# A normalized convolution over 8 images: x laid out by row and column parity, four full products per 2x2 pixel block

## The chip, the cores and the metric

The kernel runs on one core of a Trainium2 chip. The metric is the time of one execution on the device in microseconds (us), the median of several runs. Of the core's engines, TensorE (PE in the profile) multiplies matrices into PSUM and loads its weights by records of their own (PEld); VectorE (DVE) and ScalarE (ACT) work on elements; GpSimd (POOL) prepares constants; SyncE (SP) issues transfers. Sixteen DMA engines move the data.

## The reference

`x` is 8 images of 32 channels of 128 x 128 f32. `_gn` normalizes over 16 groups of two channels each; `_L0_conv_ref` convolves by transforms; the result is added to `x`:

```
def _gn(v, G=16, eps=1e-5):
    g = v.reshape(B_, G, C_ // G, H_, W_)
    m = jnp.mean(g, axis=(2, 3, 4), keepdims=True)
    s = jnp.var(g, axis=(2, 3, 4), keepdims=True)
    return ((g - m) / jnp.sqrt(s + eps)).reshape(v.shape)
def _L0_conv_ref(x, weight, bias, stride, padding):
    ...  # transforms of 256 x 256, norm='ortho'
    sh = (fft_H - out_h) // 2
    sw = (fft_W - out_w) // 2
    out = sp[:, :, sh:sh + out_h, sw:sw + out_w]
    return out + bias[None, :, None, None]
x = x + _L0_conv_ref(_gn(x), L0_conv_weight, L0_conv_bias, 1, 1)
```

The three 'ortho' transforms leave a factor of 1/256, and the crop starts at (64, 64). So with g the normalized x, `out[h, w] = x[h, w] + bias + 1/256 * sum weight[c, a, b] * g[c, 64+h-a, 64+w-b]` over channels and the 3 x 3 taps, where g is zero outside of the image. The sum reads rows and columns 62 to 127 of g and is empty for h > 65 or w > 65: only a 66 x 66 corner of each output gets a convolution, the rest is x + bias.

## The kernel before

Four images (4 x 32 channels) lie on the 128 partitions at a time, so there are two passes (`grp`, L119). All of x fits on the chip: its ten loads, five chunks of rows (CHUNKS, L54) for each pass, are issued first on the SP queue (L72). The weights come in four copies on ScalarE's queue (L80) and are put by GpSimd into block-diagonal matrices `w_bd` of 128 x 128, one for each of the nine taps (L86); three quarters of each matrix are zeros.

Each pass takes statistics of 512 elements at a time with `bn_stats` (L113, 32 instructions), joins them with `bn_aggr` (L132), and goes back and forth between engines: mean of the two channels of a group by a product with `pair` (L137), copied out and subtracted (L139, L141), variance (L143), again a product (L147), square root on ScalarE (L150), reciprocal (L152). VectorE then writes the normalized part g (L158). ScalarE adds the bias where the convolution gives nothing (L171, L175), and those rows are stored (L179).

The convolution goes block by block, each of six output rows x 66 columns = 396 elements in a PSUM bank: nine products accumulate (L192), then VectorE adds bias and x (L200). Eleven blocks make a pass. In the first pass the statistics of the second are spread behind the blocks' additions (L205). A chunk's rows are stored when its last block has been added (L206). A scheduler of the language may move instructions of an engine past each other; the lists further down show the order that results.

Of the kernel before, what the change touches and what calls it, by code (L numbers as in the profile page):

```python
# [12 lines left out]
The 1/256 is part of the normalization's factor, where it is exact.  # L13
"""
# [14 lines left out]
STATS = 512  # most elements that one bn_stats takes  # L29
BLOCK = 6  # output rows of one accumulation group in PSUM  # L30
# [3 lines left out]
def conv_preact_kernel(  # L34
# [9 lines left out]
    B, C, H, W = x.shape  # L44
    K = 3
    IMGS = P // C
    NGRP = B // IMGS
    LO = (FFT - H) // 2 - (K - 1)  # first row and column of g that the sum reads
    N = H - LO  # rows and columns that the sum reads
    NC = H + K - 1 - (FFT - H) // 2  # output rows and columns where it isn't empty  # L50
    NP = N + K - 1  # with the zeros behind the image
    # rows of the image in one load and store: a multiple of 4 (bn_stats), and chunks that
    # hold output rows of the convolution start at a multiple of BLOCK
    CHUNKS = ((0, 24), (24, 24), (48, 20), (68, 32), (100, 28))  # L54
    NSTAT = H * W // STATS
    RSTAT = STATS // W

    cpool = ctx.enter_context(tc.tile_pool(name="const", bufs=1))
    xpool = ctx.enter_context(tc.tile_pool(name="x", bufs=2))
    gpool = ctx.enter_context(tc.tile_pool(name="g", bufs=2))  # L60
# [4 lines left out]
    # all of x fits on the chip: its loads are issued at once  # L65
    xts = []
    for grp in range(NGRP):
        src = x[grp * IMGS : (grp + 1) * IMGS].rearrange("b c h w -> (b c) h w")
        tiles = []
        for i, (r0, rows) in enumerate(CHUNKS):  # L70
            xt = xpool.tile([P, rows, W], F32, tag=f"x{i}", name=f"x{grp}_{i}")
            nc.sync.dma_start(xt, src[:, r0 : r0 + rows, :])  # L72
            tiles.append(xt)
        xts.append(tiles)

    # weights and bias, once for each image on the partitions
    w_sb = cpool.tile([P, K * K, C], F32, name="w_sb")
    bias_sb = cpool.tile([P, 1], F32, name="bias_sb")
    for b in range(IMGS):
        nc.scalar.dma_start(w_sb[b * C : (b + 1) * C], weight)  # L80
        nc.scalar.dma_start(bias_sb[b * C : (b + 1) * C], bias)
    w_bd = cpool.tile([P, K * K, P], F32, name="w_bd")
    nc.gpsimd.memset(w_bd, 0.0)  # L83
    for b in range(IMGS):
        part = slice(b * C, (b + 1) * C)
        nc.gpsimd.tensor_copy(w_bd[part, :, part], w_sb[part])  # L86
# [3 lines left out]
    nc.gpsimd.memset(pair, 0.5)  # L90
# [8 lines left out]
    pair2 = pair.rearrange("p a b -> p (a b)")  # L99
    eps = cpool.tile([P, 1], F32, name="eps")  # L100
    nc.gpsimd.memset(eps, EPS * FFT * FFT)

    all_stats = [
        spool.tile([P, NSTAT, 6], F32, tag="stats", name=f"stats{grp}") for grp in range(NGRP)
    ]
    todo = [
        [(i, r0 // RSTAT, r) for i, (r0, rows) in enumerate(CHUNKS) for r in range(0, rows, RSTAT)]
        for _ in range(NGRP)
    ]

    def take_stats(grp, count):
        for i, s0, r in todo[grp][:count]:
            nc.vector.bn_stats(  # L113
                all_stats[grp][:, s0 + r // RSTAT, :],
                xts[grp][i][:, r : r + RSTAT, :].rearrange("p h w -> p (h w)"),
            )
        del todo[grp][:count]

    for grp in range(NGRP):  # L119
        tiles = xts[grp]  # L120
        dst = out[grp * IMGS : (grp + 1) * IMGS].rearrange("b c h w -> (b c) h w")

        # zeros behind the image
        g = gpool.tile([P, NP, NP], F32, tag="g", name=f"g{grp}")
        nc.gpsimd.memset(g[:, N:NP, :], 0.0)
        nc.gpsimd.memset(g[:, 0:N, N:NP], 0.0)

        # mean and variance of each channel
        take_stats(grp, NSTAT)
        stats = all_stats[grp]  # L130
        mv = spool.tile([P, 2], F32, tag="mv", name=f"mv{grp}")
        nc.vector.bn_aggr(mv, stats.rearrange("p n s -> p (n s)"))  # L132
# [3 lines left out]
        ps_m = ps_stat.tile([P, 1], F32, tag="ps_m", name=f"ps_m{grp}")  # L136
        nc.tensor.matmul(ps_m, pair2, mv[:, 0:1], start=True, stop=True)  # L137
        mean = spool.tile([P, 1], F32, tag="mean", name=f"mean{grp}")
        nc.vector.tensor_copy(mean, ps_m)  # L139
        diff = spool.tile([P, 1], F32, tag="diff", name=f"diff{grp}")  # L140
        nc.vector.tensor_sub(diff, mv[:, 0:1], mean)  # L141
        var = spool.tile([P, 1], F32, tag="var", name=f"var{grp}")
        nc.vector.scalar_tensor_tensor(  # L143
            var, in0=diff, scalar=diff, in1=mv[:, 1:2], op0=ALU.mult, op1=ALU.add
        )
        ps_v = ps_stat.tile([P, 1], F32, tag="ps_v", name=f"ps_v{grp}")
        nc.tensor.matmul(ps_v, pair2, var, start=True, stop=True)  # L147
        # 1 / (256 * sqrt(var + eps))
        std = spool.tile([P, 1], F32, tag="std", name=f"std{grp}")
        nc.scalar.activation(std, ps_v, AF.Sqrt, bias=eps, scale=float(FFT * FFT))  # L150
        rstd = spool.tile([P, 1], F32, tag="rstd", name=f"rstd{grp}")
        nc.vector.reciprocal(rstd, std)  # L152

        # the part of x that the convolution reads, normalized
        for xt, (r0, rows) in zip(tiles, CHUNKS):
            lo = max(r0, LO)
            if lo < r0 + rows:
                nc.vector.tensor_scalar(  # L158
                    g[:, lo - LO : r0 + rows - LO, 0:N],
                    xt[:, lo - r0 : rows, LO:W],  # L160
                    mean,
                    rstd,
                    ALU.subtract,
                    ALU.mult,
                )

        # x + bias where the convolution gives nothing
        for xt, (r0, rows) in reversed(list(zip(tiles, CHUNKS))):
            nrc = min(max(NC - r0, 0), rows)
            if nrc:  # L170
                nc.scalar.activation(  # L171
                    xt[:, 0:nrc, NC:W], xt[:, 0:nrc, NC:W], AF.Identity, bias=bias_sb
                )
            if nrc < rows:
                nc.scalar.activation(  # L175
                    xt[:, nrc:rows, :], xt[:, nrc:rows, :], AF.Identity, bias=bias_sb
                )
            if not nrc:
                nc.sync.dma_start(dst[:, r0 : r0 + rows, :], xt)  # L179

        # x + (convolution + bias)
        for xt, (r0, rows) in zip(tiles, CHUNKS):
            nrc = min(max(NC - r0, 0), rows)
            if not nrc:
                continue
            for r in range(0, nrc, BLOCK):
                ps = ps_conv.tile([P, BLOCK, NC], F32, tag="ps", name=f"ps{grp}_{r0 + r}")
                for a in range(K):
                    for b in range(K):
                        top = r0 + r + K - 1 - a  # L190
                        left = K - 1 - b
                        nc.tensor.matmul(  # L192
                            ps,
                            w_bd[:, a * K + b, :],
                            g[:, top : top + BLOCK, left : left + NC],
                            start=(a == 0 and b == 0),
                            stop=(a == K - 1 and b == K - 1),
                        )
                part = xt[:, r : r + BLOCK, 0:NC]
# [34 lines left out]
```

## Time and profile before

| | us |
|---|---|
| median of 3 runs | 187.21 (186.94 to 187.78) |
| span of the profiled execution | 185.6 |
| TensorE busy | 137.0 |
| VectorE busy | 61.1 |
| ScalarE busy | 25.8 |

The span runs from the first to the last instruction of the profiled execution; the runs' times lie a little above it. Busy times of different engines overlap, so what decides is the chain of work that ended last, and the waits along it. In lists of grouped instructions a row gives line, engine, operation, output and inputs, and shapes, then the busy time in all, the mean time of one in ns, and the idle time of the engine before them with what ended it. In a table of stretches each engine has its busy time and, in brackets, its instructions; then follow the granted TensorE clock (1.00 is full), the share of the DMA engines' time and GB/s.

### The profile page before, as it was taken

To read this page: it belongs to the slowest core of one execution; us is meant where nothing else is said; L and a number is where in the kernel's file an instruction comes from. 1 tells how busy PE (TensorE), PEld (TensorE's weight loads), DVE (VectorE), ACT (ScalarE), POOL (GpSimd) and SP (SyncE) were. 2 spreads that over 40 slices of the span, in tenths; PEclk is the share of its full clock that TensorE was granted. 3 is DMA by queue.
4 is the path that set the end of the run, shared out by engine and by line. 5 is a ranking of instruction groups with operands and counts; after the bars stand their busy time and mean duration, and the time that the engine had idled before them with its cause. 6 is when DMAs were issued, how large, how long until landed. Compare 5 with 4: busy or idle time off the path is not lost.

```text
span 185.6 us, 1044 instructions
## 1 busy us (share of the span) xinstructions
PE 137.0 (74%) x404; PEld 78.0 (42%) x404; DVE 61.1 (33%) x102; ACT 25.8 (14%) x16; POOL 5.2 (3%) x17
## 2 busy tenths in 40 slices
PE   0000000249999999999999929999999999999960
PEld 0000000225555555555555515555555555555530
DVE  0258799599779611101110062101110011101110
ACT  0050200379700000000000029500000000000000
POOL 4230000000000000000000000000000000000000
PEclk9999999999999999999999996999999999999997
DMA  5689999997792052000440051990007000080006
GB/s 177 231 351 446 422 425 426 432 432 308 328 407 113 4 230 109 0 0 0 170 170 0 0 212 74 396 452 0 0 42 297 0 0 4 0 339 0 0 15 267
DMA packets 3268, 33.76 MB, mean 182 GB/s; under 512 B 576, under 2 KB 704, under 8 KB 704
## 3 DMA queue, kind: packets, MB, share of 16 engines
q1 hardware_dynamic: 2880, 33.56, 43.4%
q10 hardware_dynamic: 384, 0.15, 0.4%
q8 instruction: 3, 0.05, 0.1%
q14 instruction: 1, 0.01, 0.0%
HBM read 16.93 MB, written 16.78 MB: 182 GB/s over the span
## 4 chain that ended last, share of the span: by engine, by line
PE 74%; DMA 11%; DVE 9%; issue 1%; SPq 0%; ACT 0%; ACTq 0%
PE ps L192 73%; DMA x<-x_dram 11%; DVE stats L113 6%; DVE g L158 2%; DVE x L200 1%; DVE mv L132 1%; PE ps_v L147 1%; SPq L72 0%; PE ps_m L137 0%; ACT std L150 0%; DVE var L143 0%; DVE rstd L152 0%; DVE mean L139 0%; DVE diff L141 0%; ACT L150 0%
## 5 line engine op out<-in xcount | busy, mean ns | idle before, releaser
L192 PE MATMUL ps<-g,w_bd 128*128 128x396 f32 x396 | 135.4, 504 | 6.7 <-DVE g L158 6.7
L192 PEld LDWEIGHTS ps<-g,w_bd 128*128 128x128 f32 x396 | 76.3, 193 | 64.7 <-issue 9.9
L200 DVE SCALAR_TENSOR_TENSOR x<-ps,bias_sb,x 128x396 f32<-128x396 f32 x22 | 13.9, 630 | 103.2 <-PE ps L192 103.2
L113 DVE BATCH_NORM_STATS2 stats<-x 128x6 f32<-128x512 f32 x64 | 39.0, 679 | 12.3 <-DMA x<-x_dram 12.3
L137 PE MATMUL ps_m<-mv,pair 128*128 128x1 f32 x4 | 0.8, 278 | 32.8 <-DVE mv L132 32.8
L137 PEld LDWEIGHTS ps_m<-mv,pair 128*128 128x128 f32 x4 | 0.9, 250 | 33.1 <-issue 32.8
L175 ACT ACTIVATE x<-x,bias_sb 128x256 f32<-128x256 f32 (+2 forms) x6 | 14.5, 2483 | 0.0
L171 ACT ACTIVATE x<-x,bias_sb 128x1488 f32<-128x1488 f32 (+1 forms) x6 | 8.5, 1429 | 8.3 <-DVE stats L113 6.4
L150 ACT ACTIVATE std<-ps_v,eps 128x1 f32<-128x1 f32 x2 | 0.5, 261 | 59.6 <-PE ps_v L147 59.6
L158 DVE TENSOR_SCALAR g<-x,mean,rstd 128x396 f32<-128x396 f32 (+2 forms) x6 | 5.8, 1032 | 0.0
L150 ACT ACT_TABLE_LOAD x1 | 1.3, 1283 | 15.8 <-PE ps_v L147 15.8
L147 PE MATMUL ps_v<-var,pair 128*128 128x1 f32 x4 | 0.9, 304 | 2.8 <-DVE var L143 2.8
L171 ACT ACT_TABLE_LOAD x1 | 1.3, 1283 | 9.1 <-DMA bias_sb<-bias_dram 9.1
L132 DVE BATCH_NORM_AGGREGATE mv<-stats 128x2 f32<-128x192 f32 x2 | 2.0, 1022 | 0.1
L147 PEld LDWEIGHTS ps_v<-var,pair 128*128 128x128 f32 x4 | 0.8, 249 | 3.0 <-DVE var L143 1.7
L86 POOL COPY w_bd<-w_sb 32x288 f32<-32x288 f32 x4 | 1.7, 421 | 5.1 <-DMA w_sb<-weight_dram 5.0
L152 DVE RECIPROCAL rstd<-std 128x1 f32<-128x1 f32 x2 | 0.3, 164 | 2.5 <-ACT std L150 2.5
L83 POOL MEMSET w_bd<- 128x1152 f32 x1 | 1.1, 1058 | 0.3 <-POOLq L224 0.3
L95 POOL TENSOR_SCALAR_AFFINE_SELECT pair<-pair 128x128 f32<-128x128 f32 x1 | 0.7, 706 | 0.1
L91 POOL TENSOR_SCALAR_AFFINE_SELECT pair<-pair 128x128 f32<-128x128 f32 x1 | 0.7, 706 | 0.0
L139 DVE COPY mean<-ps_m 128x1 f32<-128x1 f32 x2 | 0.3, 153 | 0.7 <-PE ps_m L137 0.7
L143 DVE SCALAR_TENSOR_TENSOR var<-diff,mv 128x1 f32<-128x1 f32 x2 | 0.4, 212 | 0.0
(9 smaller groups left out, 1.9 us busy)
## 6 DMA issues: line engine op xcount, KB each, us to landing
x<-x_dram SPq DMA_DIRECT2D x4, 1536.0 KB, 13.9
out_dram<-x SPq DMA_DIRECT2D x4, 1536.0 KB, 5.1
x<-x_dram SPq DMA_DIRECT2D x2, 2048.0 KB, 22.3
out_dram<-x SPq DMA_DIRECT2D x2, 2048.0 KB, 8.2
x<-x_dram SPq DMA_DIRECT2D x2, 1792.0 KB, 24.9
out_dram<-x SPq DMA_DIRECT2D x2, 1792.0 KB, 6.6
x<-x_dram SPq DMA_DIRECT2D x2, 1280.0 KB, 17.9
out_dram<-x SPq DMA_DIRECT2D x2, 1280.0 KB, 4.4
```

Of the source, the lines that this page charges most:

```text
L83: nc.gpsimd.memset(w_bd, 0.0)
L86: nc.gpsimd.tensor_copy(w_bd[part, :, part], w_sb[part])
L113: nc.vector.bn_stats(all_stats[grp][:, s0 + r // RSTAT, :], xts[grp][i][:, r : r + RSTAT, :].rearrange("p h w -> p (h w)"),)
L132: nc.vector.bn_aggr(mv, stats.rearrange("p n s -> p (n s)"))
L137: nc.tensor.matmul(ps_m, pair2, mv[:, 0:1], start=True, stop=True)
L147: nc.tensor.matmul(ps_v, pair2, var, start=True, stop=True)
L150: nc.scalar.activation(std, ps_v, AF.Sqrt, bias=eps, scale=float(FFT * FFT))
L158: nc.vector.tensor_scalar(g[:, lo - LO : r0 + rows - LO, 0:N], xt[:, lo - r0 : rows, LO:W], mean, rstd, ALU.subtract, ALU.mult,)
L171: nc.scalar.activation(xt[:, 0:nrc, NC:W], xt[:, 0:nrc, NC:W], AF.Identity, bias=bias_sb)
L175: nc.scalar.activation(xt[:, nrc:rows, :], xt[:, nrc:rows, :], AF.Identity, bias=bias_sb)
L192: nc.tensor.matmul(ps, w_bd[:, a * K + b, :], g[:, top : top + BLOCK, left : left + NC], start=(a == 0 and b == 0), stop=(a == K - 1 and b ...
L200: nc.vector.scalar_tensor_tensor(part, in0=ps, scalar=bias_sb, in1=part, op0=ALU.add, op1=ALU.add)
```

## The change

The host now splits x by the parity of row and column: an image becomes 128 partitions (2 row parities x 2 column parities x 32 channels) of 64 x 64 elements. A partition pitch is 16 KiB in place of 64 KiB. One image fills the partitions, and there are eight images instead of two groups of four. In this layout an output pixel block of 2 x 2 needs input blocks at two row offsets and two column offsets, so the nine taps become four products with 128 x 128 matrices, which the host builds (`blocks`) and which hold the nine taps at several places; the output corner is 33 x 33 blocks, in three chunks of 11 x 33 = 363 elements. The first image is loaded in four transfers, the others in two; each is stored in two, and the host puts the output back in order.

The mean over a group is now over eight partitions (two channels x four parities) by a product with `avg`, which VectorE builds from `pair`. ScalarE loads its root table at the start (`warm`) and does the normalizing, as scale times x plus bias, for which VectorE also computes minus mean times reciprocal. ScalarE goes on to add the bias below (1,984 elements) and right (33 x 31). `tc.manual_schedule()` keeps the order as it is written. The core of the new code:

```diff
+    for img in range(B):
+        parts = 4 if img == 0 else 2
+        for k in range(parts):
+            rows = slice(k * H // parts, (k + 1) * H // parts)
+            nc.sync.dma_start(xts[img][:, rows, :], x[img, :, rows, :])
+        if img == 0:
+            nc.sync.dma_start(w_sb, weight)
+            nc.scalar.dma_start(bias_sb, bias)
...
+    warm = cpool.tile([P, 1], F32, name="warm")
+    nc.scalar.activation(warm, eps, AF.Sqrt)
...
+    def group_mean(img):
+        ps_ms[img] = ps_stat.tile([P, 1], F32, tag="ps_m", name=f"ps_m{img}")
+        nc.tensor.matmul(ps_ms[img], avg, mvs[img][:, 0:1], start=True, stop=True)
...
+    def normalize(img):
+        xt, g = xts[img], gs[img % 2]
+
+        std = spool.tile([P, 1], F32, tag="std", name=f"std{img}")
+        nc.scalar.activation(std, ps_vs[img], AF.Sqrt, bias=eps, scale=float(FFT * FFT))
+        rstd = spool.tile([P, 2], F32, tag="rstd", name=f"rstd{img}")
+        nc.vector.reciprocal(rstd[:, 0:1], std)
+        nc.vector.scalar_tensor_tensor(
+            rstd[:, 1:2], in0=means[img][:, 0:1], scalar=-1.0, in1=rstd[:, 0:1],
+            op0=ALU.mult, op1=ALU.mult,
+        )
+        nc.scalar.activation(
+            g[:, 0:N, 0:N], xt[:, LO:H, LO:W], AF.Identity,
+            bias=rstd[:, 1:2], scale=rstd[:, 0:1],
+        )
+
+        low = xt[:, N:H, :].rearrange("p h w -> p (h w)")
+        nc.scalar.activation(low, low, AF.Identity, bias=bias_sb)
+        right = xt[:, 0:N, N:W]
+        nc.scalar.activation(right, right, AF.Identity, bias=bias_sb)
+
+    def multiply(img, n):
+        g = gs[img % 2]
+        ps = ps_conv.tile([P, ROWS, N], F32, tag="ps", name=f"ps{img}_{n}")
+        for k in range(4):
+            top, left = n * ROWS + k // 2, k % 2
+            nc.tensor.matmul(
+                ps, w_sb[:, k, :], g[:, top : top + ROWS, left : left + N],
+                start=(k == 0), stop=(k == 3),
+            )
+        return ps
...
+    take_stats(0, 0, NSTAT)
+    aggregate(0)
+    group_mean(0)
+    deviations(0)
+    group_variance(0)
+    normalize(0)
+    store(0, N, H)
+    take_stats(1, 0, NSTAT)
+    aggregate(1)
+    for img in range(B):
+        more, yet_more = img + 1 < B, img + 2 < B
+        ps = multiply(img, 0)
+        if more:
+            group_mean(img + 1)
+            deviations(img + 1)
+        add(img, 0, ps)
+        if yet_more:
+            take_stats(img + 2, 0, NSTAT // 2)
+        ps = multiply(img, 1)
+        if more:
+            group_variance(img + 1)
+            normalize(img + 1)
+            store(img + 1, N, H)
+        add(img, 1, ps)
+        if yet_more:
+            take_stats(img + 2, NSTAT // 2, NSTAT)
+            aggregate(img + 2)
+        ps = multiply(img, 2)
+        add(img, 2, ps)
+        store(img, 0, N)
...
+    with tile.TileContext(nc) as tc, tc.manual_schedule():
```

`take_stats` is `bn_stats` over 8 rows of 64 elements, `aggregate` is `bn_aggr` over 8 of them; `deviations` is copy, difference and variance as before; `group_variance` is the product with `avg` of the variance; `add` is the addition of bias and x as before; `store` is a transfer on the SP queue.

On TensorE before, at the border of the two groups, the products run in strings of nine per block (names end in a running number; `ps_54` is the block from output row 54), and the two products of the statistics stand between the groups:

```order
L192 MATMUL ps_54_307<-g_117,w_bd 128x396 x9
L192 MATMUL ps_60_321<-g_117,w_bd 128x396 x9
L137 MATMUL ps_m_340<-mv_338,pair 128x1
L147 MATMUL ps_v_348<-var_346,pair 128x1
L192 MATMUL ps_0_365<-g_335,w_bd 128x396 x9
```

After the change, on TensorE from the second to the third image (`ps_0`, `ps_1`, `ps_2` are the chunks of an image):

```order
L162 MATMUL ps_2_206<-g_116,w_sb 128x363 x4
L162 MATMUL ps_0_213<-g_119,w_sb 128x363 x4
L120 MATMUL ps_m_218<-mv_204,avg 128x1
L162 MATMUL ps_1_229<-g_119,w_sb 128x363 x4
L134 MATMUL ps_v_234<-mean_220,avg 128x1
L162 MATMUL ps_2_252<-g_119,w_sb 128x363 x4
L162 MATMUL ps_0_259<-g_116,w_sb 128x363 x4
```

Each image now has three strings of four, and the next image's two products of the statistics have moved in between them.

On VectorE before, around the second group's first blocks, nothing but additions follows the normalizing (L158), as the statistics were done in the first group:

```order
L139 COPY mean_342<-ps_m_340 128x1
L141 TENSOR_TENSOR diff_344<-mv_338,mean_342 128x1
L143 SCALAR_TENSOR_TENSOR var_346<-diff_344,mv_338 128x1
L152 RECIPROCAL rstd_352<-std_350 128x1
L158 TENSOR_SCALAR g_335<-x_2_87,mean_342,rstd_352 128x6x66
L158 TENSOR_SCALAR g_335<-x_3_89,mean_342,rstd_352 128x32x66
L158 TENSOR_SCALAR g_335<-x_4_91,mean_342,rstd_352 128x28x66
L200 SCALAR_TENSOR_TENSOR x_0_83<-ps_0_365,bias_sb,x_0_83 128x6x66
```

After the change, on VectorE during the second image's chunks (`x_73`): the third image's mean and root (`mean_220`, `rstd_238`) and the fourth image's statistics (`x_75`) stand between its additions:

```order
L125 COPY mean_220<-ps_m_218 128x1
L127 TENSOR_TENSOR mean_220<-mv_204,mean_220 128x1
L128 SCALAR_TENSOR_TENSOR mean_220<-mean_220,mv_204 128x1
L171 SCALAR_TENSOR_TENSOR x_73<-ps_0_213,bias_sb,x_73 128x11x33
L109 BN_STATS stats_125<-x_75 128x6 x4
L142 RECIPROCAL rstd_238<-std_236 128x1
L143 SCALAR_TENSOR_TENSOR rstd_238<-mean_220,rstd_238 128x1
L171 SCALAR_TENSOR_TENSOR x_73<-ps_1_229,bias_sb,x_73 128x11x33
L109 BN_STATS stats_125<-x_75 128x6 x4
L116 BN_AGGR mv_250<-stats_125 128x2
L171 SCALAR_TENSOR_TENSOR x_73<-ps_2_252,bias_sb,x_73 128x11x33
```

The normalizing has left VectorE for ScalarE, and four statistics now stand between the variance and the reciprocal of the next image.

On the SP queue before, the second load already waits for a DMA semaphore (eight of them, DMAHW0 to DMAHW7, are used in turn by SP's and ScalarE's transfers):

```order
L72 DMA x_0_73<-x_dram 128x3072
L72 DMA x_1_75<-x_dram 128x3072 [waits DMAHW1_49]
L72 DMA x_2_77<-x_dram 128x2560 [waits DMAHW2_49]
L72 DMA x_3_79<-x_dram 128x4096 [waits DMAHW3_49]
L72 DMA x_4_81<-x_dram 128x3584 [waits DMAHW4_49]
```

After the change, the start of the SP queue (`x_72` is the first image, `x_79` the last; DMAHW0 is used first by the bias):

```order
L68 DMA x_72<-x_dram 128x1024 x4
L70 DMA w_sb<-weight_dram 128x512
L68 DMA x_73<-x_dram 128x2048 x2
L68 DMA x_74<-x_dram 128x2048 [waits DMAHW0_49]
L68 DMA x_74<-x_dram 128x2048 [waits DMAHW1_49]
L68 DMA x_75<-x_dram 128x2048 [waits DMAHW2_49]
```

Seven transfers now stand ahead of the first such wait. All loads come before the first store on this queue, as before.

More of the change, by code (lines that the diff above doesn't have):

```diff
@@ L28 @@
 FFT = 256
-STATS = 512
-BLOCK = 6
+STATS = 8
 @with_exitstack
@@ L63, in conv_preact_kernel @@
     ps_stat = ctx.enter_context(tc.tile_pool(name="ps_stat", bufs=1, space=bass.MemoryType.PSUM))
[L66 to L77, printed above, removed]
-    bias_sb = cpool.tile([P, 1], F32, name="bias_sb")
[L79 to L86, printed above, removed]
+    xts = [xpool.tile([P, H, W], F32, name=f"x{img}") for img in range(B)]
+    w_sb = cpool.tile([P, 4, P], F32, name="w_sb")
+    bias_sb = cpool.tile([P, 1], F32, name="bias_sb")
+    for img in range(B):
[6 more added lines that the diff above has]
+            nc.scalar.dma_start(bias_sb, bias)
     pair = cpool.tile([P, P // 2, 2], F32, name="pair")
-    nc.gpsimd.memset(pair, 0.5)
+    nc.gpsimd.memset(pair, 0.125)
     nc.gpsimd.affine_select(
@@ L99, in conv_preact_kernel @@
     pair2 = pair.rearrange("p a b -> p (a b)")
-    eps = cpool.tile([P, 1], F32, name="eps")
[L101 to L112, printed above, removed]
+    avg = cpool.tile([P, P], F32, name="avg")
@@ L113, in take_stats @@
+    stats = [cpool.tile([P, NSTAT, 6], F32, name=f"stats{img}") for img in range(B)]
+    mvs, ps_ms, ps_vs, means = {}, {}, {}, {}
+    def take_stats(img, first, last):
+        for s in range(first, last):
             nc.vector.bn_stats(
-                all_stats[grp][:, s0 + r // RSTAT, :],
-                xts[grp][i][:, r : r + RSTAT, :].rearrange("p h w -> p (h w)"),
-            )
[L117 to L142, printed above, removed]
@@ L143, in conv_preact_kernel, with deviations @@
+    def deviations(img):
+        means[img] = spool.tile([P, 2], F32, tag="mean", name=f"mean{img}")
+        nc.vector.tensor_copy(means[img][:, 0:1], ps_ms[img])
+        diff = means[img][:, 1:2]
+        nc.vector.tensor_sub(diff, mvs[img][:, 0:1], means[img][:, 0:1])
         nc.vector.scalar_tensor_tensor(
-            var, in0=diff, scalar=diff, in1=mv[:, 1:2], op0=ALU.mult, op1=ALU.add
+            diff, in0=diff, scalar=diff, in1=mvs[img][:, 1:2], op0=ALU.mult, op1=ALU.add
         )
-        ps_v = ps_stat.tile([P, 1], F32, tag="ps_v", name=f"ps_v{grp}")
@@ L147, in conv_preact_kernel @@
[L147 to L165, printed above, removed]
@@ L168, in conv_preact_kernel @@
[L168 to L179, printed above, removed]
@@ L182, in conv_preact_kernel, with group_variance @@
[L182 to L199, printed above, removed]
-                nc.vector.scalar_tensor_tensor(
-                    part, in0=ps, scalar=bias_sb, in1=part, op0=ALU.add, op1=ALU.add
-                )
-                if grp + 1 < NGRP:
-                    take_stats(grp + 1, -(-NSTAT * BLOCK // NC))
-            nc.sync.dma_start(dst[:, r0 : r0 + rows, :], xt)
+    def group_variance(img):
+        ps_vs[img] = ps_stat.tile([P, 1], F32, tag="ps_v", name=f"ps_v{img}")
+        nc.tensor.matmul(ps_vs[img], avg, means[img][:, 1:2], start=True, stop=True)
@@ new lines, in multiply, with add @@
+    def multiply(img, n):
[8 more added lines that the diff above has]
+        return ps
+    def add(img, n, ps):
+        part = xts[img][:, n * ROWS : (n + 1) * ROWS, 0:N]
+        nc.vector.scalar_tensor_tensor(
+            part, in0=ps, scalar=bias_sb, in1=part, op0=ALU.add, op1=ALU.add
+        )
@@ new lines, in store @@
+    def store(img, first, last):
+        nc.sync.dma_start(out[img, :, first:last, :], xts[img][:, first:last, :])
+    take_stats(0, 0, NSTAT)
[28 more added lines that the diff above has]
+        store(img, 0, N)
@@ L228 @@
     ]
[L229 to L230 removed]
+    shape = arrays["x_dram"].shape
+    args.append(nc.dram_tensor("out_dram", shape, F32, kind="ExternalOutput").ap())
+    with tile.TileContext(nc) as tc, tc.manual_schedule():
         conv_preact_kernel(tc, *args)
     r = run_bass_kernel_spmd(nc, [arrays], core_ids=[0])
[L233 removed]
+    out = np.asarray(r.results[0]["out_dram"]).reshape(B, 2, 2, C, H // 2, W // 2)
+    return np.ascontiguousarray(out.transpose(0, 3, 4, 1, 5, 2)).reshape(B, C, H, W)
```

60 lines of the change are left out of this document (38 added, 22 removed).

## The prediction

> **What bounds the kernel now.** I read the spans and clock, the page's busy times and chain, then the chain in order of time, the grouped instructions, and last the transfers.
>
> ```profile
> core 0: 185.6 us, clock 0.984
> PE 137.0 (74%) x404; PEld 78.0 (42%) x404; DVE 61.1 (33%) x102; ACT 25.8 (14%) x16; POOL 5.2 (3%) x17
> PE 74%; DMA 11%; DVE 9%; issue 1%; SPq 0%; ACT 0%; ACTq 0%
> ```
>
> TensorE (PE) is the chain for 74% of the span. The chain in order of time (start, duration, what) shows how it is made up:
>
> ```profile
> 22.60 9.01 DVE stats L113 x15
> 31.61 0.02 issue
> 31.64 1.03 DVE mv L132
> ...
> 32.80 0.57 PE ps_m L137 x2
> ...
> 39.83 67.76 PE ps L192 x198
> ...
> 108.90 0.37 PE ps_v L147 x2
> ...
> 111.71 67.66 PE ps L192 x198
> ...
> 179.40 0.63 DVE x L200
> ```
>
> Nothing overlaps the two convolutions of 67.7 us except work that ends sooner: 39.8 us pass before the first (loads, statistics, normalizing), 4.1 us between them, and 5.6 us (180.03 to 185.6) behind the last addition, for its store and the end of the program. The median of the runs, 187.21 us, is 1.6 us above this execution's span; I make the sum in the span's time and add 1.6. A change under 0.5%, about 0.9 us, could not be told from none, as the runs spread by 0.84 us.
>
> **TensorE's share.** An f32 product is two records in the trace: 22 blocks x 9 taps x 2 = 396. Each convolution starts slow; weight loads (PEld), one per record, show the pitch:
>
> ```profile
> 112.51 0.34 PEld L192 LDWEIGHTS ps<-g,w_bd 128*128 128x128 f32 x1 [0.32 <-issue]
> 113.17 0.34 PEld L192 LDWEIGHTS ps<-g,w_bd 128*128 128x128 f32 x1 [0.32 <-issue]
> ...
> 115.02 4.84 PEld L192 LDWEIGHTS ps<-g,w_bd 128*128 128x128 f32 x15 [0.20 <-issue]
> 113.00:115.00 2.00, 2.00 (x4) 1.01 (x3) 0.00 (x0) 2.00 (x1) 0.00 (x0) 0.53 0.00 0
> ```
>
> At first a record comes every 0.66 us, at a granted clock of 0.53 (last but two column of the fourth row). Later 15 loads take 4.84 us; less 0.19 for the last one, that is 14 steps of 0.332 us. 198 x 0.332 = 65.7, so the slow start costs 67.66 - 65.7 = 2.0 us. The change makes 24 blocks x 4 products x 2 = 192 records of 363 columns in place of 396 of 396. By columns a record is 0.332 x 363/396 = 0.304 us (if it did not shrink: 0.332), a block of 8 records 2.43 us, an image 7.3 us, all eight 58.4 us against 131.5. So 73 us of products go, and the question is what is late next.
>
> **Vector and scalar work.** The grouped rows (busy us, mean ns) and two rows of the timeline:
>
> ```profile
> L113 DVE BATCH_NORM_STATS2 stats<-x 128x6 f32<-128x512 f32 x64 | 39.0, 679 | 12.3 <-DMA x<-x_dram 12.3
> L200 DVE SCALAR_TENSOR_TENSOR x<-ps,bias_sb,x 128x396 f32<-128x396 f32 x22 | 13.9, 630 | 103.2 <-PE ps L192 103.2
> L132 DVE BATCH_NORM_AGGREGATE mv<-stats 128x2 f32<-128x192 f32 x2 | 2.0, 1022 | 0.1
> L175 ACT ACTIVATE x<-x,bias_sb 128x4096 f32<-128x4096 f32 x2 | 7.4, 3693 | 0.0
> L171 ACT ACTIVATE x<-x,bias_sb 128x1116 f32<-128x1116 f32 x2 | 2.5, 1228 | 2.0 <-DVE g L158 2.0
> 47.76 0.63 DVE L200 SCALAR_TENSOR_TENSOR x<-ps,bias_sb,x 128x396 f32<-128x396 f32 x1 [1.59 <-PE ps L192]
> 48.31 4.24 DVE L113 BATCH_NORM_STATS2 stats<-x 128x6 f32<-128x512 f32 x7
> 108.16 0.15 DVE L139 COPY mean<-ps_m 128x1 f32<-128x1 f32 x1
> 108.34 0.16 DVE L141 TENSOR_TENSOR diff<-mv,mean 128x1 f32<-128x1 f32 x1
> 108.54 0.22 DVE L143 SCALAR_TENSOR_TENSOR var<-diff,mv 128x1 f32<-128x1 f32 x1
> 109.29 0.26 ACT L150 ACTIVATE std<-ps_v,eps 128x1 f32<-128x1 f32 x1 [59.62 <-PE ps_v L147]
> 109.59 0.16 DVE L152 RECIPROCAL rstd<-std 128x1 f32<-128x1 f32 x1 [0.83 <-ACT std L150]
> ```
>
> Statistics stay 64 instructions of 512 elements, one per 0.60 us (15 in 9.01 us), so 2.4 us for four and 4.8 us per image. An addition (363 elements in place of 396) lets the next start after 0.55 us (47.76 to 48.31). Mean, difference and variance take 0.60 us (108.16 to 108.76). Reciprocal and the new scaled product, priced like the variance's row, take 0.4 us with their waits. The aggregate reads 48 numbers in place of 192: between 0.15 us (the copy's row) and the old 1.02; I take 0.35, near a quarter. That is 0.60 + 0.55 + 2.4 + 0.4 + 0.55 + 2.4 + 0.35 + 0.55 = 7.8 us of VectorE per image.
> ScalarE now normalizes (1,089 elements, by the 1,116 row 1.21 us), adds the bias below (1,984: 1.94, on the line between 1,116 and 4,096) and at the right (1,023: 1.15): with the root 4.6 us per image. Bias work follows the normalizing, so only stores wait for it. Its cover is 3.7 us of each period; without that it would add its excess to every period.
> The two one-column products per image now stand inside the stream of blocks. Alone they took 0.37 us warm; in the stream they could cost nothing beyond it (0.3 each) or add both weight loads (0.7). I take 0.45, near the row, as the next block's weights must also be loaded: TensorE needs 7.3 + 0.9 = 8.2 us per image, 7.9 to 8.7.
>
> **The loop's period.** Three engines of nearly equal load feed each other in a fixed order, so I follow the longest circle. From the mean's product of image i+1: the product 0.37, mean to variance 0.60 with 0.02 before it, addition of block 0 0.55, four statistics 2.4, reciprocal and product 0.4, normalizing 1.21 and hand-over 0.05, hand-over to TensorE 0.14, block 0 of image i+1 2.43, exposed weight load 0.1, then the mean's product of i+2: 8.3 us. This wait is the change's own: four statistics, queued on VectorE ahead of the reciprocal, delay normalizing, and behind the reciprocal stand the addition and four more statistics; TensorE's next block waits for all of it. TensorE alone gives 8.2, VectorE 7.8. I take 8.3.
>
> **The transfers.** Rows for the first 12 us in slices of 0.3 us, the steady load, a store phase, a lone store, the last stores' size and time to landing, and two waits:
>
> ```profile
> GB/s 0 0 0 0 0 0 410 164 93 131 403 191 444 417 410 410 328 532 369 369 492 222 204 116 35 0 0 0 0 123 451 82 41 328 287 614 205 492 369 369
> DMA packets 1213, 14.21 MB, mean 418 GB/s; under 512 B 142, under 2 KB 142, under 8 KB 142
> 48.00:54.00 6.00, 6.00 (x20) 3.42 (x19) 4.80 (x9) 1.68 (x2) 0.00 (x0) 1.00 1.04 440
> 181.40:182.40 1.00, 0.00 (x0) 0.00 (x0) 0.00 (x0) 0.00 (x0) 0.00 (x0) 1.00 0.81 338
> out_dram<-x SPq DMA_DIRECT2D x2, 1280.0 KB, 4.4
> SPq L72 <- DMA x<-x_dram: 9.4, 2, 6.8
> 8.02 3.66 DVE L113 BATCH_NORM_STATS2 stats<-x 128x6 f32<-128x512 f32 x6 [8.02 <-DMA x<-x_dram]
> ```
>
> Data flow from 1.8 us. Around 7 to 9 us they stop: the second load waited 6.8 us in the SP queue behind a reused DMA semaphore. After the change seven transfers, 4.4 MB or 10.6 us at 418 GB/s, are issued before the first such wait, which is for the bias; I cost it at nothing, and 2 us (the old hole) if the bias came that late. An image is 2.10 MB, 5.0 us; bytes of x_0 had passed by 7 us and its reader started at 8.02, so landing trails by 1 us.
> Image 0 has landed at 1.8 + 5.0 + 1 = 7.8. Its last two statistics end at 9.0, aggregate 9.35, mean's product 10.05 (0.13 + 0.57), variance 10.65, its product 11.3, root 11.6, reciprocal and product 12.0, normalizing 13.25. GpSimd's and VectorE's set-up, now without the weight copies, lies beside the load; uncovered it would be about 1 us. Block 0 ends at 13.25 + 2.43 + 2.0 (slow start) = 17.7. Image 1's statistics, loaded by about 13.5 us, are done at 17, so nothing is late there. Then 0.45 + 0.6 + 0.55 + 2.4 + 0.4 + 1.25 + 0.15 bring block 0 of image 1 to 23.5; TensorE's own work (0.45 + 2.43 + 0.45 + 2.43) gives the same. Six periods: 73.3. Image 7: 7.3, to 80.6; addition: 81.25. The last store is 1.08 MB in place of 1.31, 0.55 us less, so the end follows 5.0 us later: 86.3 us of span, and **88.0 us** with the 1.6.
>
> **Rivals.** (1) The transfers bind. 33.8 MB at 418 GB/s are 80.9 us, with 1.8 before, 1 of landing, 1.1 us from there to the span's end (the last store was issued at 180.05 and landed 4.4 us later) and 1.6: **86.4**; with stores at 440 84.4. For it: the store before last is due at 80 us and the queue is ahead by about 1 us only. Against: the last additions come later still. It holds if the period is 8.1 or less.
> (2) In-order waits stretch the circle. Each extra 0.1 us costs 0.7 us. If the aggregate stays at 1.02 us VectorE alone needs 8.5; with 0.7 us per small product TensorE needs 8.7; both and hand-overs on each of some ten crossings could make 9.0 to 10: **93 to 100**.
> (3) Smaller transfers are slower. The lone store's 338 GB/s gives 33.8/0.338 = 100 us, with 5.5 around it **105.5**. Against it: queued transfers ran at 418 and 440, and here they are queued. [...]
> (4) TensorE's clock falls in every image. After the 4.1 us between the convolutions, broken only by small products, the clock was 0.53 and the start cost 2.0 us; eight starts in place of one add 14: **102**. Against: the longest idle stretch that I find in a period is under 0.5 us. [...]
> (5) Slower than before: rows of 8 KB at steps of 16 KB (12 to 16 KB at 64 KB before) are served like the small pieces at the start, where slices show 93 to 164 GB/s. It decides from 33.8 MB / (187.2 - 5.5 us) = 186 GB/s down; at 164 it gives 206 + 5.5 = **212**. Nothing but those slices, with 1,152-byte pieces among them, speaks for it.
>
> **Chances.** Forecast 0.50 (87 to 90), (1) 0.18, (2) 0.17, (3) 0.06, (4) 0.05, (5) 0.02, and 0.02 for a start some microseconds later. 85 to 97 holds the forecast, (1) but its edge, and more than half of (2): 0.80. Only (5) is not faster by more than 0.5%; I leave 0.01 for no difference.
>
> **What would show it.** Right: TensorE busy about 8 us in each 8.3 from 23 us on, one cold start at 13 us, VectorE idle under 1 us per image, loads done near 44 us, and a chain that changes engine within each image. Wrong: additions that wait for products by microseconds (TensorE alone binds), 16 DMA engines full to the end (rival 1), a clock row below 0.9 after 20 us (rival 4), or rates under 400 GB/s while stores are queued (rival 3).

## The result, and the profile after

The changed kernel takes 90.06 us (median of 4 runs, 89.69 to 90.71) against 187.49 us before: a ratio of 0.481, 95% interval 0.478 to 0.483. It lies in the predicted range of 85 to 97, 2.1 us above the predicted 88.0 and just outside of the narrower 87 to 90 that the forecast gave to its own sum. Its profiled execution spans 88.2 us. The times of the experiments below are medians of a kernel's fast executions; those more than 1.5% above its fastest (two with the packed bias, one each with two transfers and with the doubled product) are left out, as they are from the ratios. Clock, busy times and shares of the chain:

```profile
core 0: 88.2 us, clock 0.994
PE 67.2 (76%) x224; PEld 41.5 (47%) x224; DVE 60.6 (69%) x142; ACT 37.9 (43%) x34; POOL 2.1 (2%) x11
PE 76%; DMA 8%; DVE 7%; ACT 2%; issue 1%; SPq 0%; DVEq 0%
```

TensorE's busy time has halved, VectorE's is what it was, and TensorE still has 76% of the chain: that share alone would say that it is bound by its products as before. The chain in order of time (start, duration, what; ps_m and ps_v are the one-column products of the mean and the variance) has to be read piece by piece:

```profile
15.03 1.31 ACT g L147
16.34 0.04 issue
16.38 5.21 PE ps L162 x8
21.59 0.22 PE ps_m L120 x2
21.81 2.79 PE ps L162 x8
...
29.70 0.11 PE ps_m L120 x2
29.81 2.55 PE ps L162 x8
32.36 0.12 PE ps_v L134 x2
32.48 5.22 PE ps L162 x16
37.70 0.12 PE ps_m L120 x2
...
72.50 9.89 PE ps L162 x32
...
82.48 0.60 DVE x L171
```

The last 32 records, with nothing between them, take 9.89 us, 0.309 us each: 2.47 for a block of 8, 4.94 for 16. Block 0 of image 0 takes 5.21. From image to image (29.70 to 37.70) the period is 8.00 us. In it, the string of 16 that crosses to the next image takes 5.22, so 0.28 more than its products.

What happens in such a crossing, from the timeline of one period (start, duration, engine, line, operation, and in brackets the idle time before it):

```profile
37.85 0.16 DVE L125 COPY mean<-ps_m 128x1 f32<-128x1 f32 x1 [0.52 <-PE ps_m L120]
38.88 2.46 DVE L109 BATCH_NORM_STATS2 stats<-x 128x6 f32<-128x512 f32 x4
41.26 0.15 DVE L142 RECIPROCAL rstd<-std 128x1 f32<-128x1 f32 x1
41.64 1.31 ACT L147 ACTIVATE g<-x,rstd 128x1089 f32<-128x1089 f32 x1 [0.86 <-DVE rstd L143]
43.00 2.13 PEld L162 LDWEIGHTS ps<-g,w_sb 128*128 128x128 f32 x8 [0.55 <-ACT g L147]
45.86 0.16 DVE L125 COPY mean<-ps_m 128x1 f32<-128x1 f32 x1 [0.52 <-PE ps_m L120]
```

VectorE goes from the mean through four statistics to the reciprocal without a gap, ScalarE waits for the reciprocal, and the weight load of the next image's first block waits 0.55 us for ScalarE. These rows close a circle: 1.03 us from the copy (37.85) to the statistics (38.88), 2.38 to the reciprocal, 0.38 to the normalizing, 1.36 to the weight load, and 2.86 through block 0 and the next mean's product to the next copy (45.86), 8.01 us together. The chain of waits books the weight load's wait as TensorE's, because the ends of its products are modelled.

The transfers by stretches (last two columns: share of the DMA engines' time, GB/s):

```profile
4.00:5.00 1.00, 0.00 (x0) 0.00 (x0) 0.00 (x0) 0.00 (x0) 0.00 (x0) 1.00 0.63 148
6.00:7.00 1.00, 0.00 (x0) 0.00 (x0) 0.41 (x1) 0.00 (x0) 0.00 (x0) 1.00 1.01 414
76.00:78.00 2.00, 2.00 (x8) 1.20 (x7) 0.47 (x1) 1.55 (x2) 0.00 (x0) 1.00 0.67 279
82.00:84.00 2.00, 0.37 (x2) 0.00 (x0) 0.60 (x1) 0.00 (x0) 0.00 (x0) 1.00 0.26 106
```

They start slowly until 6 us, run without a gap until 76, and then have two gaps of 0.7 and 1.5 us (the missing shares of two stretches of 2 us): the transfers were 2.2 us from being the bound.

### The profile page after: what moved, and what is told of

Its sections match the earlier page's. It is cut to its first block, busy times and chain, and to the rows that moved or that the text cites. A ratio compares the mean times of both kernels' runs of the same rounds, so it can differ in the third digit from the quotient of the medians.

```text
span 88.2 us, 744 instructions
## 1 busy us (share of the span) xinstructions
PE 67.2 (76%) x224; PEld 41.5 (47%) x224; DVE 60.6 (69%) x142; ACT 37.9 (43%) x34; POOL 2.1 (2%) x11
## 4 chain that ended last, share of the span: by engine, by line
PE 76%; DMA 8%; DVE 7%; ACT 2%; issue 1%; SPq 0%; DVEq 0%
PE ps L162 73%; DMA x<-x_dram 8%; DVE stats L109 4%; PE ps_m L120 2%; PE ps_v L134 2%; ACT g L147 1%; DVE x L171 1%; DVE mv L116 0%; SPq L68 0%; ACT std L140 0%; DVE mean L128 0%; DVE rstd L142 0%; DVE rstd L143 0%; DVE mean L127 0%; DVE mean L125 0%
## 5 line engine op out<-in xcount | busy, mean ns | idle before, releaser
L162 PE MATMUL ps<-g,w_sb 128*128 128x363 f32 x192 | 65.9, 493 | 2.1 <-ACT g L147 2.1
L162 PEld LDWEIGHTS ps<-g,w_sb 128*128 128x128 f32 x192 | 36.1, 197 | 23.5 <-ACT g L147 5.2
L171 DVE SCALAR_TENSOR_TENSOR x<-ps,bias_sb,x 128x363 f32<-128x363 f32 x24 | 13.8, 576 | 7.0 <-PE ps L162 7.0
L153 ACT ACTIVATE x<-x,bias_sb 128x1984 f32<-128x1984 f32 x8 | 15.6, 1949 | 0.3
L147 ACT ACTIVATE g<-x,rstd 128x1089 f32<-128x1089 f32 x8 | 10.4, 1305 | 5.8 <-DVE rstd L143 4.9
L120 PE MATMUL ps_m<-mv,avg 128*128 128x1 f32 x16 | 2.7, 236 | 12.4 <-DVE mv L116 12.4
L120 PEld LDWEIGHTS ps_m<-mv,avg 128*128 128x128 f32 x16 | 3.4, 222 | 14.4 <-DVE mv L116 12.4
L155 ACT ACTIVATE x<-x,bias_sb 128x1023 f32<-128x1023 f32 x8 | 9.1, 1132 | 0.0
L134 PEld LDWEIGHTS ps_v<-mean,avg 128*128 128x128 f32 x16 | 3.1, 204 | 2.4 <-DVE mean L128 0.8
L116 DVE BATCH_NORM_AGGREGATE mv<-stats 128x2 f32<-128x48 f32 x8 | 3.0, 372 | 0.3
```

The lines of the kernel that those rows point to most:

```text
L116: nc.vector.bn_aggr(mvs[img], stats[img].rearrange("p n s -> p (n s)"))
L120: nc.tensor.matmul(ps_ms[img], avg, mvs[img][:, 0:1], start=True, stop=True)
L134: nc.tensor.matmul(ps_vs[img], avg, means[img][:, 1:2], start=True, stop=True)
L147: nc.scalar.activation(g[:, 0:N, 0:N], xt[:, LO:H, LO:W], AF.Identity, bias=rstd[:, 1:2], scale=rstd[:, 0:1],)
L153: nc.scalar.activation(low, low, AF.Identity, bias=bias_sb)
L155: nc.scalar.activation(right, right, AF.Identity, bias=bias_sb)
```

## The experiments

The theory: a circle through all engines, with four statistics in it, sets the period; the bias's pieces slow the first loads (148 GB/s from 4 to 5 us, 414 from 6 to 7); the transfers stand just behind. The main rival: TensorE's own instructions set the period.

**The bias packed with the weights.** The host appends the bias as a column to the weights.

```diff
-    w_sb = cpool.tile([P, 4, P], F32, name="w_sb")
-    bias_sb = cpool.tile([P, 1], F32, name="bias_sb")
+    wb_sb = cpool.tile([P, 4 * P + 1], F32, name="wb_sb")
+    w_sb = wb_sb[:, 0 : 4 * P].rearrange("p (k q) -> p k q", k=4)
+    bias_sb = wb_sb[:, 4 * P : 4 * P + 1]
...
-            nc.sync.dma_start(w_sb, weight)
-            nc.scalar.dma_start(bias_sb, bias)
+            nc.sync.dma_start(wb_sb, weight)
...
```

> The bias comes as one more column of the weights' transfer, so the transfer of 128 pieces of 4 bytes on ScalarE's queue is gone; nothing else changes. Theory (those small pieces slow the load from 2 to 6 us, where the changed kernel's rows show 131 to 283 GB/s): over 350 GB/s from 3 us on, image 0's first statistics start near 4 us in place of 6.6, block 0 starts at 13 to 14 us in place of 16.4, and the time falls by 2.5 to 3 us to about 87. Rival (any first transfers are slow): rows of 2 to 6 us stay below 300 GB/s and the time stays at 90.0 within 0.5.

Measured 88.26 us (87.93 to 88.67), ratio 0.472 (0.470 to 0.473). Two stretches of the start (DMA share and GB/s last):

```profile
3.00:4.00 1.00, 0.00 (x0) 0.00 (x0) 0.38 (x5) 0.20 (x1) 0.00 (x0) 1.00 0.80 217
4.00:5.00 1.00, 0.00 (x0) 0.00 (x0) 0.00 (x0) 0.00 (x0) 0.00 (x0) 1.00 0.98 393
```

From 4 us on the load is fast (393 in place of 148), and block 0 starts at 15.04 us, 1.3 us earlier. That is half of what was expected: the rates of 2 to 4 us stay low (217). The time falls by 1.8 us; the rest of it is no gain of the load, as blocks 0 and 1 of image 0 happened to take 4.71 and 2.55 us here in place of 5.21 and 2.79. The pieces are one cause of the loads' slow start and not the only one.

**Image 0 in two transfers in place of four.** Rows of 8 KiB in place of 4.

```diff
-        parts = 4 if img == 0 else 2
+        parts = 2
```

> Image 0 is loaded in two transfers with rows of 8 KiB in place of four with 4 KiB. If rows of 4 KiB are what slows the start, the rows of 2 to 6 us come near 400 GB/s and the time falls by 2 to 3 us to 87 to 88. Theory (the bias's pieces are the cause): the rates of 2 to 6 us stay under 300 GB/s; the first statistics wait for 1 MiB in place of 0.5, so the start comes up to 1 us later and the time is 90 to 91.

Measured 88.97 us (88.59 to 89.8), ratio 0.476 (0.474 to 0.478). The same stretch of 4 to 5 us:

```profile
4.00:5.00 1.00, 0.00 (x0) 0.00 (x0) 0.00 (x0) 0.00 (x0) 0.00 (x0) 1.00 0.92 303
```

Neither expectation holds: in this stretch the rate doubles with the row's size, from 148 to 303, without reaching 393, and over the whole of 2 to 6 us its mean rises from 187 to 266. In the profiled execution, the longest of the four, block 0 starts only 0.3 us earlier (16.11); where the others gain the microsecond is not shown. That each row of x takes turns with a piece of the bias is the author's assumption, made for the last of the packed runs below: no run shows turns. What is shown is that larger rows lost less beside the pieces (303 against 148 GB/s), and that run finds the row's size to matter without the pieces too (352 against 225 GB/s from 3 to 4 us).

**Three statistics ahead of the reciprocal, five behind it.**

```diff
-            take_stats(img + 2, 0, NSTAT // 2)
+            take_stats(img + 2, 0, 3)
...
-            take_stats(img + 2, NSTAT // 2, NSTAT)
+            take_stats(img + 2, 3, NSTAT)
```

> Three statistics in place of four stand ahead of the reciprocal, five behind the addition; the work is the same. Theory (the circle through VectorE sets the period of 8.0 us): normalizing ends 0.6 us earlier, TensorE no longer waits for it, and the period falls to TensorE's own 7.75 to 7.8, so block 0 of the last image starts 1.2 to 1.5 us earlier and the time falls by about that, to 88.5 to 89. Rival (TensorE alone sets the period of 8.0): the period stays at 8.0 and the time at 90.0 within 0.5.

Measured 88.92 us (88.42 to 89.33), ratio 0.475 (0.473 to 0.477). The chain in the middle and at the end:

```profile
36.16 0.12 PE ps_m L120 x2
...
38.94 4.99 PE ps L162 x16
43.93 0.11 PE ps_m L120 x2
...
80.00 0.60 DVE x L171
```

And the transfers at the end:

```profile
80.00:82.00 2.00, 0.00 (x0) 0.00 (x0) 0.60 (x1) 0.00 (x0) 0.00 (x0) 1.00 0.94 397
82.00:84.00 2.00, 0.00 (x0) 0.00 (x0) 0.00 (x0) 0.00 (x0) 0.00 (x0) 1.00 0.97 406
```

The string of 16 falls to 4.99, and the period to 7.77 us with the same instructions on each engine: the circle, not TensorE's load, had set it. The last addition starts 2.5 us earlier than in the changed kernel (80.00 against 82.48). Five crossings that are 0.23 us shorter give 1.2 of that; the rest is the start, where blocks 0 and 1 of image 0 happened to take 4.42 and 2.55 us in place of 5.21 and 2.79. So the period decides here and not the time, and the span is only 1.2 us shorter, 87.0. The DMA engines are now busy after the last addition too: the transfers end it.

**A one-column product made twice.**

```diff
-        nc.tensor.matmul(ps_vs[img], avg, means[img][:, 1:2], start=True, stop=True)
+        for _ in range(2 if img else 1):
+            nc.tensor.matmul(ps_vs[img], avg, means[img][:, 1:2], start=True, stop=True)
```

> The variance's one-column product is made twice for images 1 to 7; the second repeats the first. It costs TensorE 0.12 to 0.3 us per image where, by the circle, TensorE has about 0.25 us to spare. Theory (circle): the period stays at 8.0 to 8.1 and the time within 0.5 us of 90.0. Rival (TensorE alone): the period grows by the whole cost, to 8.15 to 8.3, and the time by 1 to 2 us, to 91 to 92.

Measured 89.82 us (89.17 to 90.08), ratio 0.479 (0.478 to 0.481). The chain:

```profile
37.24 0.12 PE ps_m L120 x2
37.35 2.55 PE ps L163 x8
39.90 0.34 PE ps_v L135 x4
40.24 5.00 PE ps L163 x16
45.24 0.12 PE ps_m L120 x2
```

TensorE does 0.22 us more per image (0.34 in place of 0.12), the string behind it takes 0.22 less, and the period stays at 8.00. The rival falls: TensorE had that time to spare.

**One product per block.**

```diff
-        for k in range(4):
+        for k in (0,):
...
-                start=(k == 0), stop=(k == 3),
+                start=True, stop=True,
```

> Each block makes one product in place of four; three of the four products are left out of the computation. TensorE falls to a quarter. Theory (behind the circle stand the transfers, which had only 2 us of idle time near the end): additions end near 75 us, but the DMA engines are then busy without a gap, the span is 86 to 86.5 us and the time 88 to 88.5: three quarters of the products are worth about 2 us. Rival (the changed kernel is still bound by TensorE's products): the time falls by 5 us or more, to 85 or less.

Measured 88.19 us (88.14 to 88.36), ratio 0.471 (0.469 to 0.472). The last addition ends at 75.24 us, and behind it the transfers go on:

```profile
76.00:78.00 2.00, 0.00 (x0) 0.00 (x0) 0.00 (x0) 0.00 (x0) 0.00 (x0) 1.00 1.00 423
82.00:84.00 2.00, 0.00 (x0) 0.00 (x0) 0.00 (x0) 0.00 (x0) 0.00 (x0) 1.00 0.90 380
```

The kernel spans 86.6 us: from 75.2 to about 84 us the core does nothing but store. With three quarters of the remaining products gone the time falls by 1.9 us. This is the floor that the transfers set, with the slow start of the loads in it.

**Nine products per block.**

```diff
-        for k in range(4):
+        for j in range(9):
+            k = j % 4
             top, left = n * ROWS + k // 2, k % 2
...
-                start=(k == 0), stop=(k == 3),
+                start=(j == 0), stop=(j == 8),
```

> Each block makes nine products in place of four (matrices 1 to 4 used in turn, so the sums are not the convolution): 24 blocks of 363 columns and nine products are 78,408 columns, as many as 22 of 396 and nine before. This leaves of the change all but the smaller number of products. Theory (products and order add up): TensorE needs 16.9 us per image, the span is 16.4 + 2 + 8 x 16.9 + 5 = 159 and the time about 160, so the order by images brings 27 us and the products 70. Rival (the order brings nothing by itself): 180 to 190.

Measured 160.82 us (160.15 to 161.78), ratio 0.859 (0.855 to 0.862). The chain, for one period:

```profile
40.11 0.12 PE ps_m L120 x2
...
45.94 11.09 PE ps L163 x36
57.04 0.12 PE ps_m L120 x2
```

The period is 16.9 us, and TensorE is bound by its products: a string of 36 takes 0.308 us a record. All that the change does besides, with as many columns of products as before, is worth 27 us (187.6 to 160.8): order by images, layout, loads and normalizing on ScalarE together, which no run takes apart. Having four products in place of nine is worth the other 71 (160.8 to 90.1).

**Packed bias and three statistics together; then image 0 in two transfers as well.** The edits are those above.

> The bias packed with the weights and three statistics ahead of the reciprocal, together. Theory: additions end near 79.3 us, but then the transfers bind: without their idle 1.2 us of the run with the packed bias alone the span is 85.0 to 85.3 us and the time 87.0 to 87.4. Rival (both gains add up in full): 88.6 - 1.6 = 87.0 less another half a microsecond, 86.0 to 86.5, with a gap left in the transfers.

> As the kernel with the packed bias and three statistics, with image 0 also loaded in two transfers (rows of 8 KiB in place of 4). If rows of 4 KiB alone are slow at the start, the rows of 2 to 4 us rise from 220 to 240 GB/s to over 350 and the time falls by 0.7 us more, to 86.3 to 86.7. Theory (rows of 4 KiB were slow only because each took turns with a piece of the bias): within 0.4 us of the run before it.

Measured 88.21 us (87.71 to 88.95), ratio 0.472 (0.469 to 0.474), and 87.2 us (86.73 to 88.02), ratio 0.465 (0.463 to 0.468). Neither came as expected. In the first, additions ended at 81.02 us and not at 79.3, since blocks 0 and 1 of image 0 took 5.21 and 3.00 us: from 16.05 to 20.28 us a weight load came every 0.60 us. The gains do not add up, and the size of the slow start differs from run to run (4.42 us for block 0 in the run with three statistics, 4.71 with the packed bias, 5.21 here and in the changed kernel). The second is 1.0 us faster by time, but its profiled execution has nearly the same span (86.2 against 86.3). That one is the longest of its six executions (84.9 to 86.2 us, against 86.0 to 87.0 for the first), so the microsecond lies within the span, but no trace shows where. What the two traces do show is the load from 3 to 4 us, the first kernel's row and then the second's:

```profile
3.00:4.00 1.00, 0.00 (x0) 0.00 (x0) 0.39 (x5) 0.20 (x1) 0.00 (x0) 1.00 0.75 225
3.00:4.00 1.00, 0.00 (x0) 0.00 (x0) 0.39 (x5) 0.20 (x1) 0.00 (x0) 1.00 0.86 352
```

From 5 to 7 us it also runs at 426 and 418 GB/s in place of 356 and 332, while 2 to 3 us stay slow (180, before 201). So against the theory, four transfers with rows of 4 KiB are slower at the start than two with 8 KiB without the bias's pieces too. In these two executions nothing came of it: image 0's last statistics end at 11.21 us in place of 10.89.

**TensorE kept warm.** Products on constants fill TensorE's idle time before image 0.

```diff
+    def warm_up(n, name):
+        ps = ps_conv.tile([P, ROWS, N], F32, tag="ps", name=name)
+        flat = ps.rearrange("p r n -> p (r n)")
+        for _ in range(n):
+            nc.tensor.matmul(flat[:, 0:P], avg, pair2, start=True, stop=True)
+
+    warm_up(26, "warm_a")
     take_stats(0, 0, NSTAT)
...
     group_variance(0)
+    warm_up(8, "warm_b")
```

> The changed kernel with 26 products of 128 columns on constants ahead of the first statistics' product and 8 between the variance's product of image 0 and its block 0; nothing reads their results. Theory (the slow clock costs blocks 0 and 1 of image 0 2.5 to 3 us, 5.2 and 2.8 us in place of 2.43 each): block 0 takes 2.4 to 2.6 us, additions end up to 2.8 us earlier; the transfers have 2.2 us of gaps left near the end, so the time falls by 1.5 to 2.2 us, to 87.9 to 88.6. Rival (image 1's statistics, not the clock, hold up the start: they end at 20.15 us): mean and addition of image 1 wait for them, block 1 starts at 20.5 in place of 21.7, and the time falls by 1.2 us at most, to 88.9 or more.

Measured 88.57 us (88.33 to 89.0), ratio 0.472 (0.470 to 0.475). The timeline at the start:

```profile
15.62 2.71 PE L162 MATMUL ps<-g,w_sb 128*128 128x363 f32 x8 [0.18 <-ACT g L147]
19.02 0.37 DVE L116 BATCH_NORM_AGGREGATE mv<-stats 128x2 f32<-128x48 f32 x1
19.45 0.38 PE L120 MATMUL ps_m<-mv,avg 128*128 128x1 f32 x2 [1.11 <-DVE mv L116]
```

Block 0 takes 2.71 us in place of 5.21, and then the rival's wait is there as well: TensorE stands idle 1.1 us for image 1's statistics. The slow start had cost some 2.5 us on block 0, of which the statistics would have taken 1.1 anyway. Block 0 also starts 0.8 us earlier (15.62 against 16.38), in part because the two one-column products ahead of it take 0.40 us each in place of 0.60. About 1.5 us of time are gained, at the upper end of the theory's range and 0.3 below the rival's; the timeline shows that both parts are real.

**The same in the fastest kernel, and with the last store in three.**

```diff
         add(img, 0, ps)
+        if not more:
+            store(img, 0, ROWS)
...
         add(img, 1, ps)
+        if not more:
+            store(img, ROWS, 2 * ROWS)
...
-        store(img, 0, N)
+        store(img, 0 if more else 2 * ROWS, N)
```

> The fastest kernel so far (packed bias, three statistics ahead of the reciprocal, image 0 in two transfers; 87.2) with the same idle products ahead. Theory: additions end 1 to 2.8 us earlier, and the transfers' 1.9 us of gaps close, so the time is 85.3 to 86.2. Rival (the transfers bind already): within 0.4 us of 87.2.

> As the run before it, and the last image's upper rows are stored in three parts, each behind its own addition. The last store is then 0.36 MB in place of 1.08. If the transfers' queue is empty when the last addition ends, the tail of 5 us is 1.7 us shorter and the time 83.6 to 84.5; if the transfers bind by then, the gain is under 0.5 us, 85 to 86.

Measured 86.92 us (86.85 to 87.03), ratio 0.463 (0.461 to 0.465), and 87.24 us (87.18 to 87.5), ratio 0.465 (0.463 to 0.467). The expected 85.3 to 86.2 was missed: additions end 1.6 us earlier than in the kernel without warming (79.62 against 81.25), and the time is the same within its spread. With the stores in three the last addition ends at 79.07 us, and the transfers read:

```profile
78.00:80.00 2.00, 0.35 (x2) 0.00 (x0) 0.60 (x1) 0.00 (x0) 0.00 (x0) 1.00 0.98 412
80.00:82.00 2.00, 0.00 (x0) 0.00 (x0) 0.00 (x0) 0.00 (x0) 0.00 (x0) 1.00 1.00 401
```

The DMA engines work through to 83 us, so smaller last stores bring nothing (the time is 0.3 us longer): the transfers bind at 86.9 to 87.2 us. The kernel of 86.92 us is the fastest of the study, 0.463 of before against 0.481 for the change.

## Why the prediction was right, point by point

- **Sign and size.** Products: 0.304 us per record expected, 0.309 measured; the nine-product run confirms about 71 us for the products, near the 73 expected. The other 27 are what the change does besides; the runs do not take it apart.
- **The period.** 8.3 expected, 8.00 measured, by the mechanism that was named: the circle through four statistics, shown by the two runs that move one statistic and add one product. Each of its steps came out a little shorter, most of all the one from the copy of the mean to the statistics (1.03 us in place of 0.60 + 0.55). In TensorE's own sum the one-column product was too large, 0.45 each: with the circle shortened the period is 7.77, less 24 x 0.309 = 7.42 leaves 0.35, so 0.18 each, and the doubled product costs 0.22; both are below the range of 0.3 to 0.7. TensorE alone was put at 8.2 and is at most 7.77. So the sums set the circle only 0.1 us above TensorE, less than the error in TensorE's sum; that this error lay on the side that left the circle ahead was luck. The chain does not change engine within an image, which was named as a sign of being right: the profile books the wait as TensorE's, and only the rows of the timeline and the added product show the circle. VectorE was put at 7.8 and has 7.5 (8.01 less its 0.52 of idle time). The aggregate was right (0.35 expected), normalizing took 1.31 us in place of 1.21 (busy us and mean ns behind the bar):

```profile
L147 ACT ACTIVATE g<-x,rstd 128x1089 f32<-128x1089 f32 x8 | 10.4, 1305 | 5.8 <-DVE rstd L143 4.9
L116 DVE BATCH_NORM_AGGREGATE mv<-stats 128x2 f32<-128x48 f32 x8 | 3.0, 372 | 0.3
```

- **The start: the term that was mis-sized.** Image 0's normalizing was to end at 13.25 and ended at 16.34; the load of image 0 was taken at 418 GB/s from 1.8 us, and the bias at nothing unless SP waited for its semaphore. The rows of before that show 93 to 164 GB/s beside small pieces were used for the rival (5) alone and not for the first image's load, to which they applied. The packed bias brought block 0 forward by 1.3 us; from 3 to 4 us the size of the rows, or the number of transfers, has a part as well, and what slows 2 to 3 us was not settled.
- **The slow start of the products.** 2.0 us expected for the first blocks; 5.21 + 2.79 - 2 x 2.47 = 3.1 measured, with a weight load every 0.60 us at a granted clock of 1.00 in the profile. The warm run shows that 1.1 of it would have gone to image 1's statistics. The sum said that nothing is late there; with block 0 at 2.7 us, as in the warm run, it would have been wrong.
- **The sum.** Block 0 of image 1 at 27.0 in place of 23.5 (+3.5), six periods of 8.00 in place of 8.3 (-1.8), end of the products to end of the span 0.2 longer, 1.9 in place of 1.6 us around the span (+0.3): the 87.9 that the terms gave, rounded to 88.0 there, become 90.1. Two errors of opposite sign made the point look better than its terms.
- **Rivals.** (1), the transfers, was put at 86.4 and found at 86.9 to 88.2, according to the start. It was to hold from a period of 8.1 us down; at 8.00 it did not yet, because the start came 3.5 us late, and it holds once some 2 us are saved anywhere. (2) did not come: hand-overs took 0.02 to 0.05 us. (3) fell: in the stretches of 2 us from 6 to 76 us the rates lie between 401 and 442 GB/s with transfers of 1 MB. (4) fell: after 24 us no string of 16 records takes longer than 5.23 us, where 16 at twice the pitch of 0.309 us would take 9.9. (5) fell with (3).

## What to carry to other kernels

When a bound falls by half, sum every other engine and the transfers for one period before believing the gain, and follow the circle of dependences through the fixed order: here TensorE's 7.8, the circle's 8.0 and VectorE's 7.5 us per image, and the transfers over the whole span, lay so close together that each later saving of 1 to 3 us was cut short by the next of them. A busy share in the chain does not say that an engine is the bound; adding work to it and seeing no change does say that it is not. A small constant that would run beside the first load is worth trying as part of a larger transfer: here the first load went from 148 to 393 GB/s between 4 and 5 us with the bias as a column of the weights, and the time fell by 1.8 us, in part by chance.

## What the runs showed of the hardware that was not expected

One transfer of 128 pieces of 4 bytes on another queue brought the first loads from 393 to 148 GB/s in the stretch from 4 to 5 us, and the loss depended on the rows that it ran beside (with two transfers and rows of 8 KiB 303, and 426 without the pieces).

The clock column (the last but two) did not show the slow start of the changed kernel: it reads 1.00 over the stretch in which weight loads, in the timeline below it, come every 0.60 us in place of 0.31:

```profile
16.38:21.60 5.22, 5.22 (x10) 3.07 (x10) 3.74 (x7) 2.97 (x2) 0.00 (x0) 1.00 1.02 424
```

```profile
17.15 0.34 PEld L162 LDWEIGHTS ps<-g,w_sb 128*128 128x128 f32 x1 [0.27 <-issue]
17.76 0.34 PEld L162 LDWEIGHTS ps<-g,w_sb 128*128 128x128 f32 x1 [0.27 <-issue]
```

The slow start differs from run to run: weight loads of the first products came at the slow pitch for 3.2 us with three statistics (16.20 to 19.39), 3.8 us with the packed bias (15.04 to 18.84) and 5.0 us in the changed kernel (16.38 to 21.38). What sets that length was not shown. With it gone the runs of a kernel lie closer together (86.85 to 87.03 us with the products on constants, 86.73 to 88.02 without), though the transfers, which bind in the kernel with them, may explain that as well.
